# Three edits to the order of work around the routing stage of an attention and mixture-of-experts kernel: running sums one unit of projections sooner, one unit more behind the fifth group of one-hot rows, last keys' activations one product later

## The chip, the cores and the metric

The kernel runs on one core of one Trainium2 chip. The metric is the device time of one execution in microseconds (us). The core has five engines that run their own instruction streams in order and wait for each other by semaphores: PE (TensorE, the matrix products; its weight loads are shown as PEld), DVE (VectorE), ACT (ScalarE), POOL (GpSimd) and SP (SyncE, which only issues DMAs here). ACT and POOL issue DMAs too.

## The reference, cut to what matters

The input x has 2 x 2048 tokens of 512 channels. It is normalised, xn = layernorm(x); the attention layer normalises xn once more with gamma and beta.

```python
# attention, on xn, causal, one head of width 512
x_norm = (xn - mu) / sqrt(var + EPS) * gamma + beta
q, k, v = x_norm @ Wq, x_norm @ Wk, x_norm @ Wv
s = softmax(mask(q @ k.T / sqrt(512))) @ v @ o_proj + xn
# mixture of 8 experts on xn, the best 2 of each token
scores = xn @ gate_w.T + gate_b + bias
top_scores, top_idx = top_k(scores, 2)
comb = sum(one_hot(top_idx, 8) * softmax(top_scores))
h = silu(einsum('td,ehd->teh', xn, w1) + b1)
y = einsum('teh,edh->ted', h, w2) + b2
out = x + s * silu(einsum('ted,te->td', y, comb))
```

## The kernel before, in words

**Stages.** The tokens are cut into 32 tiles of 128, and the tiles into 8 blocks of 512 tokens (`NB` = 8). The first stage, to about 256 us, normalises each block, turns it so that the channels lie on the partitions (`zT`), applies gamma and beta (`kT`, the keys), and multiplies it by two folded weights: `wqk` (query times key weights) and `wvo` (value times output weights). The results go to DRAM. In the same stage the scores of the experts are made, and near its end the routing: each token's two experts, its place in the list of its expert, and the inverse list `toki`, which says which token lies in which slot. From about 256 to 570 us the experts run over the slots, whose rows POOL gathers by `toki`. The rest is attention and the output.

**Products.** The projections of blocks 0 to 6 use seven products of half size in place of eight. `items` lists (block, weight) pairs, 14 of them, and `chain_of_products` gives the order (i, k) of the products: the seven k of neighbouring items are interleaved, so that a bank's copies lie behind another product. `one_product(i, k)` issues four matmuls of 128 x 256 in float32 into one of four PSUM banks (`bank_a` to `bank_d`, line 465) and then ACT's copies:

- k = 1 writes bank_a. k = 2 adds to bank_a, which is copied out (line 491).
- k = 5 writes bank_d, which ACT copies to a tile `p5` (line 488, `FIFTH`).
- k = 6 adds to bank_b, and ACT copies bank_b to bank_c (line 494).
- k = 3 adds to bank_b, which is copied out (line 478), and bank_b is loaded with the next item's bank_a (line 499). k = 7 and k = 4 add to bank_c (lines 478 and 508).

The outputs of k = 3 and k = 7 still lack the fifth product. DVE adds it (line 330), an instruction that `deferred` holds back until two more products have been issued (`add_due`).

**Units.** The generator `pieces` yields after one or two products, four units for seven products; the units of block 7 are whole products instead, four matmuls of 128 x 512 (lines 381 and 386). There are 64 units. Whatever is put in between is placed by counting units: `next(projected)` issues one more. The instructions stand in the program in just this order (`manual_schedule`), so an engine meets its work in the order in which the Python code issued it.

**Keys.** `keys(b)` turns a block with DVE copies (line 307), and puts the four activations `scaled` (ACT, line 312), one for each quarter of the channels, into `pending`, with the number of the product from which they may be issued. After each product `scale_next` issues one that is due. The last of the four also issues the DMA that stores the keys to `kt_d`, on ACT's queue.

**Routing.** `route()` is a generator. It starts when 41 of the 64 units are out, and each `yield n` lets n more units be issued before it goes on. First come constants (POOL, lines 531 to 556) and the choice of the two experts (DVE, lines 566 to 595), which ends with the matrix `chosen`. Then two small matmuls, `cum` and `tot_p` (lines 599 and 601), give running sums over the tokens of a tile and sums of each tile, and about 30 DVE instructions (lines 603 to 673) make from them the slot of each choice. Then the inverse list: for each of the two choices (k = 0, 1) and each of four groups of eight tiles (t0 = 0, 8, 16, 24), DVE builds one-hot rows `at`, `mine` and `which` (lines 706 to 717), and `invert()` issues eight bf16 matmuls on PE that add the group into `inv_p` (line 684). The fifth group is k = 1, t0 = 0. The tiles `at` and `which` lie in the pool `hot` with two buffers, so the third group after a given one can be built only when PE has used the given one. After the last group `inv_p` is turned into `toki` (line 731), and POOL gathers the first slots (line 883).

```python
groups.append((at, which, k, t0))
if k == 0 or t0 + GROUP < NT:
    yield 1
invert()
```

The lines of `route` up to its end consume 4 + 5 + 4 + 3 + 1 = 17 units; the rest of the 64 are issued with the first steps of the experts.

Of the kernel before, what the change touches and what calls it, by code (L numbers as in the profile page):

```python
# [26 lines left out]
def gated_attention_moe(  # L27
# [35 lines left out]
    NB = NT // BT  # L63
# [231 lines left out]
    def keys(b):  # L295
        zs = zs_of.pop(b)
        zT = ztp.tile([P, ND, TB], F32, name=f"zT_{b}", tag="zT")
        kT = kp.tile([P, ND, TB], F32, name=f"kT_{b}", tag="kT")
        if b < BY_TE:
            for c in range(ND):  # L300
                pt = ps_t.tile([P, TB], F32, name=f"pz_{b}_{c}", tag="pt")
                for t in range(BT):
                    nc.tensor.transpose(pt[:, ts(t, P)], zs[t][:, ts(c, P)], ident)
                nc.scalar.copy(zT[:, c, :], pt)
        else:
            for t in range(BT):
                nc.vector.tensor_copy(
                    zT[:, :, ts(t, P)].bitcast(U16).rearrange("p c (t h) -> p c t h", h=2),
                    zuts.pop((b, t)).rearrange("p (h c) t -> p c t h", h=2),
                )  # L310
        def scaled(c):
            nc.scalar.activation(
                kT[:, c, :], zT[:, c, :], AF.Identity,
                scale=gam[:, c : c + 1], bias=bet[:, c : c + 1],
            )
            if c == ND - 1:
                nc.scalar.dma_start(out=kt_d[b], in_=kT)

        wait = made[0] + (3 if b in (1, NB - 1) else 6)
        pending.extend((wait, scaled, c, b) for c in range(ND))  # L320
        if b < BY_TE:
            scale_all()
        kts[b], zts[b] = kT, zT

    made, pending, deferred = [0], [], []
# [11 lines left out]
    def scale_all():  # L337
        while pending:
            _, f, c, _ = pending.pop(0)
            f(c)  # L340
# [179 lines left out]
    def route():  # L520

        with ExitStack() as rt:
# [46 lines left out]
            def over_e(dst, src, op):  # L569
                nc.vector.tensor_reduce(dst, src.rearrange("p e t -> p t e"), AX.X, op)  # L570
# [23 lines left out]
            chosen = rp.tile(G, BF16, name="chosen")  # L594
            nc.vector.tensor_tensor(chosen, oh1, oh2, ALU.add)
            flat = chosen.rearrange("p e t -> p (e t)")
            yield 4
            cum = ps_r.tile([P, E * NT], F32, name="cum")
            nc.tensor.matmul(cum, lhsT=tri, rhs=flat, start=True, stop=True)
            tot_p = ps_r.tile([P, E * NT], F32, name="tot_p")  # L600
# [80 lines left out]
            def invert():  # L681
                at, which, k, t0 = groups.pop()
                for i in range(GROUP):
                    nc.tensor.matmul(
                        inv_p, lhsT=at[:, i, :], rhs=which[:, i, :, :],
                        start=(k == 0 and t0 + i == 0), stop=(k == 1 and t0 + i == NT - 1),
                    )

            for k, oh in enumerate((oh1, oh2)):
                nc.vector.tensor_tensor(oh, oh, excl, ALU.mult)  # L690
                pos = rp.tile([P, NT], F32, name=f"pos{k}")
                over_e(pos, oh, ALU.add)
                nc.vector.tensor_copy(posi[k], pos)
                parts_i = rp.tile([P, 2, NT], I32, name=f"parts_i{k}")
                nc.vector.tensor_scalar(
                    parts_i[:, 0, :], posi[k], 7, None, ALU.arith_shift_right
                )
                nc.vector.tensor_scalar(parts_i[:, 1, :], posi[k], P - 1, None, ALU.bitwise_and)
                part = rp.tile([P, 2, NT], BF16, name=f"part{k}")
                nc.vector.tensor_copy(part, parts_i)  # L700
                for t0 in range(0, NT, GROUP):
                    def along(v, n):
                        return v[:, t0 : t0 + GROUP].unsqueeze(2).to_broadcast([P, GROUP, n])

                    at = hot.tile([P, GROUP, P], BF16, name=f"at_{k}_{t0}", tag="at")
                    nc.vector.tensor_tensor(  # L706
                        at, lane.unsqueeze(1).to_broadcast([P, GROUP, P]),
                        along(part[:, 1, :], P), ALU.is_equal,
                    )
                    mine = hot.tile([P, GROUP, NSP], BF16, name=f"mine_{k}_{t0}", tag="mine")  # L710
                    nc.vector.tensor_tensor(
                        mine, slot_b.unsqueeze(1).to_broadcast([P, GROUP, NSP]),
                        along(part[:, 0, :], NSP), ALU.is_equal,
                    )
                    which = hot.tile([P, GROUP, 2, NSP], BF16, name=f"which_{k}_{t0}", tag="which")
                    for i in range(2):
                        nc.vector.tensor_tensor(
                            which[:, :, i, :], mine, along(tok[i], NSP), ALU.mult
                        )
                    groups.append((at, which, k, t0))  # L720
                    if k == 0 or t0 + GROUP < NT:
                        yield 1
                    invert()
            yield 1
            inv = rp.tile([P, 2, NSP], F32, name="inv")
# [62 lines left out]
    for b in range(1, NB):  # L788
        at = begin[b]
        put(at, keys, b)  # L790
        put(at + 3, both, b)
        put(at + (4 if b == NB - 1 else 7), keep_scores, b)
        if b > 1:

            before = begin[b - 1] if b > 2 else 0
            put(max(before - 1, 0), norm_stats, b)
            put(before + 1, norm_roots, b)
            put(before + 1, norm_rows, b)
            if b + 2 < NB:

                put(before + 4, load, b + 2)
# [17 lines left out]
    norm(0)  # L819
    fold(wqk, parts[0], parts[1], 1.0 / math.sqrt(KEY))  # L820
    keys(0)
    key_sums(0)
    weight_sums(wqk, "q")
# [68 lines left out]
    for n in route():  # L892
        for _ in range(n):
            next(projected)
            done += 1
            for f, args in between.pop(done, []):
                f(*args)
            sum_keys(done)
            if done >= W2_FROM:
                load_w2(w2_left.pop(0))  # L900
# [430 lines left out]
    for i in range(NS):  # L1331
# [21 lines left out]
        for _ in range(3):  # L1353
            if i >= paired.stop and early:
                f, b, c = early.pop(0)
# [303 lines left out]
    for s in range(NT + OUT + 2):  # L1659
# [15 lines left out]
        for k in range(NT):  # L1675
            if k not in AHEAD:
                wait = 4 - k % 2 if k // 2 in FAST else 3
# [162 lines left out]
```

## Time and profile before

| | |
|---|---|
| three runs | 1026.64, 1028.63, 1025.37 us; median 1026.64 |
| the profiled execution | 1028.63 us, of which the span from first to last instruction is 1026.9 |
| mean granted PE clock | 0.998 of full speed |
| busy PE, DVE, POOL, ACT | 1015.6, 713.9, 479.9, 408.9 us |
| moved by DMA | 209.42 MB, 204 GB/s on average |

The busy time is a share of the span. A busy PE alone says nothing of the stage; the waits of PE, the chain of waits that ended last, and the windows of PE's clock say where it stood still or ran slowly. Times inside the program are in us from the start of the span.

### The profile page before, as it was taken

The numbers are of one execution on the slowest core, as the hardware profiler recorded it, in microseconds if no ns is written. First come the engines' busy times: TensorE is split into PE (matmuls) and PEld (weight loads), VectorE is DVE, ScalarE is ACT, GpSimd is POOL, SyncE is SP. The second block draws the span as 40 slices with busy tenths as digits, with TensorE's granted clock in tenths as the row PEclk, the third lists the DMA queues.
The fourth block names the chain that finished last, engine by engine and source line by source line (L and its number), as shares of the span: only waits on it lengthen the run. The fifth ranks groups of instructions, "written<-read, shape, count | busy, mean of one in ns | idle before, by whom it ended". The sixth has DMA issues, their size and how long they took to land.

```text
span 1026.9 us, 13492 instructions
## 1 busy us (share of the span) xinstructions
PE 1015.6 (99%) x3956; PEld 666.4 (65%) x3956; DVE 713.9 (70%) x1395; ACT 408.9 (40%) x817; POOL 479.9 (47%) x479
## 2 busy tenths in 40 slices
PE   9999999989999999999999999999999999999998
PEld 5688887864577667766754347687675544447577
DVE  5777746795887777677734559787577556888667
ACT  3344444322444444354445322122335553542341
POOL 3364564003744444444431237254556776754272
PEclk9999999999999999999999999999999999999999
DMA  8698995988899999999999567454768769653371
GB/s 297 204 260 287 294 276 239 343 276 184 189 231 219 203 215 223 189 228 216 221 200 237 158 208 168 110 123 136 201 174 238 230 189 251 186 136 116 97 162 42
DMA packets 299367, 209.42 MB, mean 204 GB/s; under 512 B 234392, under 2 KB 247448, under 8 KB 298272
## 3 DMA queue, kind: packets, MB, share of 16 engines
q1 hardware_dynamic: 283840, 156.09, 61.4%
q0 software_dynamic: 10560, 35.17, 13.1%
q10 hardware_dynamic: 4896, 17.30, 4.5%
q8 instruction: 34, 0.56, 0.2%
q14 instruction: 37, 0.30, 0.1%
HBM read 92.89 MB, written 60.03 MB: 149 GB/s over the span
## 4 chain that ended last, share of the span: by engine, by line
PE 90%; DVE 3%; issue 3%; SPq 1%; DMA 1%; POOL 1%; ACT 0%; ACTq 0%; POOLq 0%; DVEq 0%
PE py L1107 15%; PE ps L1219 13%; PE p L1482 12%; PE p L1050 10%; PE p L1271 8%; PE po L1434 6%; PE bank_a L465 4%; PE bank_b L465 4%; PE bank_c L465 4%; PE p L1434 3%; PE bank_d L465 2%; PE ph L998 2%; DMA y_d<-y 1%; PE bank_a L219 1%; DVE at L706 1%
## 5 line engine op out<-in xcount | busy, mean ns | idle before, releaser
L1107 PE MATMUL py<-arena,ht 128*128 (+3 forms) x408 | 182.3, 593 | 0.0
L1219 PE MATMUL ps<-k,q 128*128 128x512 f32 (+3 forms) x416 | 143.0, 495 | 0.0
L1394 POOL COPY pu<-pT 128x1024 uint16<-128x1024 uint16 (+2 forms) x74 | 82.4, 1147 | 118.3 <-ACT pT L1384 58.6
L1078 POOL COPY hu<-h 128x704 uint16<-128x704 uint16 x68 | 63.0, 946 | 155.9 <-issue 121.6
L1107 PEld LDWEIGHTS py<-arena,ht 128*128 128x128 f32 (+3 forms) x408 | 73.3, 183 | 82.2 <-issue 77.2
L1219 PEld LDWEIGHTS ps<-k,q 128*128 128x128 f32 x416 | 74.6, 190 | 66.8 <-issue 57.4
L883 POOL DMA_INDIRECT xs<-zu_d,toki x68 | 79.5, 1169 | 72.7 <-DVE toki L731 57.8
L1093 ACT ACTIVATE ht<-ht,b1sel 128x128 f32<-128x128 f32 (+3 forms) x228 | 71.1, 378 | 99.0 <-DVE ht L1087 99.0
L1057 DVE TENSOR_TENSOR h<-p,h 128x176 f32<-128x176 f32 x182 | 55.5, 337 | 53.8 <-PE p L1050 50.0
L1577 POOL DMA_INDIRECT yg<-y_d,posi x64 | 67.7, 1059 | 36.6 <-DVE yg L1588 21.1
L1434 PE MATMUL po<-v,pT 128*128 128x512 f32 x152 | 67.8, 592 | 0.0
L280 POOL COPY zu<-z 128x1024 uint16<-128x1024 uint16 x32 | 38.0, 1187 | 60.8 <-DVE z L265 60.8
L1384 ACT ACTIVATE pT<-pT,nm 128x1024 f32<-128x1024 f32 x14 | 16.1, 1148 | 110.2 <-DVE nm L1307 71.2
L1416 DVE COPY pT<-puT 128x1024 uint16<-128x1024 uint16 (+2 forms) x74 | 53.3, 749 | 7.6 <-DMA puT<-pu 7.5
L1115 ACT COPY y<-py 128x512 f32<-128x512 f32 x55 | 32.1, 584 | 59.7 <-PE py L1107 44.2
L1384 ACT ACTIVATE pT<-ps,nm 128x512 f32<-128x512 f32 (+3 forms) x52 | 30.0, 581 | 61.3 <-DVE nm L1307 37.6
L958 DVE COPY xT<-xhT 128x1024 uint16<-128x1024 uint16 x68 | 47.0, 713 | 6.2 <-DMA xhT<-xs 5.7
L1277 DVE TENSOR_TENSOR pT<-p,pT 128x512 f32<-128x512 f32 x49 | 32.8, 686 | 26.0 <-PE p L1271 22.3
L1434 PEld LDWEIGHTS po<-v,pT 128*128 128x128 f32 x152 | 28.6, 190 | 31.9 <-issue 30.1
L1606 POOL TENSOR_TENSOR o<-o,yg 128x512 f32<-128x512 f32 x30 | 41.4, 1381 | 14.3 <-DVE o L1598 14.2
L1087 DVE COPY ht<-huT 128x768 uint16<-128x768 uint16 x68 | 39.4, 579 | 12.5 <-DMA huT<-hu 12.2
L1598 DVE SCALAR_TENSOR_TENSOR o<-xo,xscale,o 128x512 f32<-128x512 f32 x30 | 27.3, 918 | 28.7 <-ACT o L1595 28.7
(323 smaller groups left out, 2159.3 us busy)
## 6 DMA issues: line engine op xcount, KB each, us to landing
y_d<-y SPq DMA_DIRECT2D x68, 256.0 KB
zu_d<-zu SPq DMA_DIRECT2D x32, 264.0 KB
kt_d<-kT ACTq DMA_DIRECT2D x8, 1024.0 KB
k<-kt_d SPq DMA_DIRECT2D x32, 256.0 KB
q<-qt_d SPq DMA_DIRECT2D x32, 256.0 KB
v<-v_d SPq DMA_DIRECT2D x32, 256.0 KB
xo<-in_x_dram SPq DMA_DIRECT2D x32, 256.0 KB
x<-in_x_dram SPq DMA_DIRECT2D x30, 256.0 KB
```

What stands on the lines that cost most here:

```text
L465: nc.tensor.matmul(ps[:, r, :], lhsT=lhs[:, c, ts(r, P)], rhs=rhs[:, c, :], start=(start and r + c == 0), stop=(c == 1), skip_group_check= ...
L883: nc.gpsimd.indirect_dma_start(out=xs, out_offset=None, in_=zu_d, in_offset=bass.IndirectOffsetOnAxis(ap=toki[:, order[i] : order[i] + 1], ...
L1050: nc.tensor.matmul(ps, lhsT=x[:, c], rhs=y(c).rearrange("p o h -> p (o h)"), start=(c == 0), stop=(c == ND // 2 - 1),)
L1078: nc.gpsimd.tensor_copy(hu[:, :, :H], h.bitcast(U16).rearrange("p (d h) -> p h d", h=2))
L1093: nc.scalar.activation(ht[:hn, c, at], ht[:hn, c, at], AF.Silu, bias=b1sel[:hn, c, j : j + 1])
L1107: nc.tensor.matmul(py[at, :], lhsT=ht[:k, c, at], rhs=rhs[n], start=(c == 0), stop=(c == NH - 1),)
L1219: nc.tensor.matmul(ps[:, :w], lhsT=aqs[seq[s] // 2][:, c, ts(t % 2, P)], rhs=aks[first + j][:, c, :w], start=(c == 0), stop=(c == ND - 1),)
L1271: nc.tensor.matmul(ps, lhsT=x[:, c], rhs=y[:, c], start=(c == 0), stop=(c == ND // 2 - 1))
L1394: nc.gpsimd.tensor_copy(pu[:, : 2 * w].rearrange("p (h d) -> p h d", h=2), turned[s][:, k : k + w].bitcast(U16).rearrange("p (d h) -> p h ...
L1434: nc.tensor.matmul(dst, lhsT=turned[s][:, ts(k, P)], rhs=avs[first + k // BT][:, k % BT, cols], start=(start and k == k0), stop=(k == k1 - 1),
L1482: nc.tensor.matmul(dst, lhsT=a[:, k], rhs=v(k), start=(k == 0), stop=(stop and k == n - 1))
L1577: nc.gpsimd.indirect_dma_start(out=y, out_offset=None, in_=y_d, in_offset=bass.IndirectOffsetOnAxis(ap=posi[k][:, n : n + 1], axis=0),)
```

## The change

The change moves work and adds or removes none. It has three places.

```diff
@@ keys(b)
-        wait = made[0] + (3 if b in (1, NB - 1) else 6)
+        wait = made[0] + {1: 3, NB - 1: 4}.get(b, 6)
@@ route(), behind `chosen`
-            yield 4
+            yield 3
             cum = ps_r.tile([P, E * NT], F32, name="cum")
@@ route(), the groups of one-hot rows
                     if k == 0 or t0 + GROUP < NT:
-                        yield 1
+                        yield 2 if k + t0 == 1 else 1
                     invert()
```

The first lets the activations of the last block's keys be issued from the fourth product after `keys(7)` on, where it was the third. The second lets three units be issued between `chosen` and the two small matmuls of the running sums, where it was four. So everything behind them in `route` stands one unit sooner, until the third place: after the rows of the fifth group (k + t0 is 1 only for k = 1, t0 = 0) two units are issued before its matmuls, where it was one. Groups five to eight stand where they stood, and the units consumed by `route` are 3 + 5 + 4 + 4 + 1 = 17 as before.

In the instructions as built, the streams of POOL and SP are in the same order. On PE, `cum` and `tot_p` stand ahead of two products that they stood behind, groups one to four stand one unit sooner, and two products on bank_b, k = 6 and k = 3 of the last item, follow each other with no group in between. On DVE the two adds of p_10 (line 330) come behind the running sums in place of ahead of them, and the two of p_12 behind the rows of the fourth group in place of ahead of them. On ACT the copy of line 494 comes ahead of the first activation of block 7's keys, and the fourth of them, with its DMA, behind the copies of lines 355 and 478.

## The prediction

> **What bounds the kernel now.** I read, in this order, the busy shares and the chain of waits of the page, then the waits of PE alone between 140 and 275 us, then the timeline there. The first two say that PE is the bound over the whole span:
>
> ```profile
> PE 1015.6 (99%) x3956; PEld 666.4 (65%) x3956; DVE 713.9 (70%) x1395; ACT 408.9 (40%) x817; POOL 479.9 (47%) x479
> ...
> PE 90%; DVE 3%; issue 3%; SPq 1%; DMA 1%; POOL 1%; ACT 0%; ACTq 0%; POOLq 0%; DVEq 0%
> ```
>
> So an edit counts only if it changes a time in which PE stands still, or PE's clock. The waits of PE in the stage of the change (us in all, times, longest):
>
> ```profile
> PE inv_p L684 <- DVE which L717: 2.2, 1, 2.2
> PE bank_b L465 <- ACT bank_c L494: 1.4, 2, 1.2
> PE bank_c L465 <- ACT so L478: 0.3, 1, 0.3
> ```
>
> The long one of the second kind, in the timeline (start, length, engine, then idle time before it and who ended it):
>
> ```profile
> 163.71 0.81 ACT L312 ACTIVATE kT<-zT,bet,gam 128x512 f32<-128x512 f32 x1 [3.11 <-DVE zT L307]
> ...
> 164.43 0.57 ACT L494 COPY bank_c<-bank_b 128x512 f32<-128x512 f32 x1
> ...
> 165.06 1.99 PE L465 MATMUL bank_b<-arena,kT 128*128 128x256 f32 x8 [1.19 <-ACT bank_c L494]
> ```
>
> ACT stands 3.11 us before a key activation that needs zT from DVE, and the copy that PE needs stands behind it. The other wait, in the chain and in PE's clock (PEclk, third column from the right):
>
> ```profile
> 228.00 1.37 DVE which L717 x2
> 229.37 0.04 issue
> 229.41 0.63 PE inv_p L684 x8
> 230.05 5.18 PE bank_c L381 x8
> 235.23 3.43 PE bank_d L381 x8
> ```
>
> ```profile
> 230.00:231.00 1.00, 1.00 (x4) 0.36 (x4) 0.85 (x4) 0.00 (x0) 0.00 (x0) 0.81 1.02 410
> 231.00:232.00 1.00, 1.00 (x3) 0.48 (x2) 0.96 (x2) 0.00 (x0) 0.83 (x1) 0.50 0.56 213
> ...
> 233.00:234.00 1.00, 1.00 (x2) 0.34 (x2) 0.97 (x2) 0.00 (x0) 1.00 (x1) 0.50 0.64 148
> 234.00:235.00 1.00, 1.00 (x3) 0.38 (x2) 0.93 (x3) 0.00 (x0) 0.69 (x2) 0.98 0.66 177
> ```
>
> DVE builds one-hot rows without a pause up to 229.36 (26.5 us busy of the 28 from 198 to 226), PE waits 2.16 us for the eighth group, and then runs at half clock: the first unit takes 5.18 where the next takes 3.43, so 1.75 us more. From 255.7 to 556 PE then never waits, so what is won before 255.7 is kept.
>
> **What the Trainium skill says.** "TensorE: Matmul & The Clock Gate", Part 1 (the HAM clock gate), says that the array falls to half clock after an idle window of about 3.4 us, counted in windows that run free of the kernel. The trace agrees on the half (0.50) and about on its length, but a gap of 2.16 us was enough here, while the gap of 1.36 us at 163.7 left the clock at 1.00. The same page's "Architectural detail" calls ACT and DVE strict FIFO; the ACT lines above agree.
>
> **The change, part by part.** All times are on the clock of the profiled execution. Durations are its own; I lay them in the order in which the changed program stands on each engine.
>
> *Key activations one product later.* In ACT's order the copy L494 now comes ahead of all four activations of b = 7. Its source is ready near 161.7 (PE left it at 161.54), so it ends near 162.3, before PE wants it at 161.97 + 1.73 = 163.70. The wait 163.70 to 165.06 goes: 1.36, and with it the slower start of the next product (1.92 to the next start instead of 1.73, 0.19): **1.55 us** sooner for PE. What is late next: the fourth activation and its DMA kt_d on ACT's queue come behind the copy of bank_c, ending near 169.7 instead of 169.0. The units of b = 7 read it from 223 on, so they do not feel it; POOL's constants (L531, 170.81 now) reuse its space, so they start near 169.8, 1.0 sooner and not 1.55. DVE's choice of experts hangs on them: `chosen` ends at 181.24 - 1.0 = 180.2.
>
> *Running sums one unit sooner.* cum and tot_p (0.11 us each) move ahead of two products (2 x 1.73 = 3.45). Now they start at 186.07, 4.8 us after `chosen`; then at 186.07 - 3.45 - 1.55 = 181.1, still 0.9 after `chosen`, so PE gets no new wait. DVE's running sums (186.49 to 195.69, 9.2 us) end near 190.7, 5.0 sooner. But their successors are then late: the two adds of the fifth product (L330 on so_10, 1.3 us, moved behind the sums), and the two of p_11, of which the second needs ACT's copy of bank_c, 195.13 + 0.59 = 195.72 now, 194.15 then. L690 follows 0.6 later: near 194.75 instead of 196.81. So DVE gains **2.1**, not 5.0. The moved adds feed a store that waits for both at 194.08 now; they are done at 192.0, so ACT's queue is not held.
>
> *Groups 1 to 4 one unit sooner on PE.* Group 1 comes to 205.29 - 3.45 - 1.55 = 200.3, its rows end at 201.91 - 2.1 = 199.8: no wait. Groups 2, 3, 4 come to 204.2, 206.5, 210.4; their rows are ready at 203.0, 206.2 and 209.4 (the adds of p_12, 1.2 us, move behind group 4). `hot` has two buffers, so DVE's third group waits for group 1 on PE: 0.89 us at 205.96 now, nothing then (group 1 is through at 201.0, DVE comes at 203.0). DVE gains **0.9** more, 3.0 in all. Both new margins of 0.3 to 0.5 us bound the error: at worst 0.5 is lost, at best nothing.
>
> *One unit more behind the fifth group.* With no group between the last two products on bank_b, PE sees the whole copy chain between them: 0.2 + 0.57 + 0.06 = 0.84 us idle, where a group of 0.47 stood in part of it. Queued behind: everything on PE, and so group 5, which comes near 218.7 (its rows are ready at 215.7). DVE's seventh group needs group 5 through, 218.7 + 0.47 + 0.2 = 219.4, and arrives at 222.35 - 3.0 = 219.35. No row of before shows this wait; I take **0.1** lost, between 0 and 0.6 (PE's starts there are good to some half us). The end of the rows is then 229.36 - 2.9 = 226.4; PE comes to the eighth group near 225.9, so it still waits, some 0.6 us, and the group starts **2.95 us** sooner, near 226.45.
>
> *Clock.* A gap of 0.6 us, and 0.84 at 214.8, are both below the 1.36 that left the clock alone: the 1.75 us of half clock go. Sum on the profiled execution: 2.95 + 1.75 = **4.7 us**.
>
> *Behind it.* The order on SP and POOL is the same, with the same DMAs. toki comes 2.95 sooner, PE's first expert product 4.7 sooner (251.0). xT for it is ready at 244.47 + 0.76 now, so 8 us of slack remain after losing 1.75. The DMA-laden stage from 516 to 570, where PE waits 1.4 us, is paced by PE's own progress: zero, with 1 us either way.
>
> **Time.** The profiled execution took 1028.63, of which 1026.9 is span: 1028.63 - 4.7 = 1023.9. It is the slowest of three runs; the others, 1026.64 and 1025.37, are lower by about what the half clock costs or more. If they lack it (an estimate, since their clock is not shown), the median gains 2.95: 1023.7. Over such runs, one in three with the half clock, the gain is 2.95 + 0.6 = 3.5 us off a mean of 1026.88, 1023.3. I take **1023.5**.
>
> **Rivals.** Measurements of this kernel can tell about 0.3%, 3.1 us, from no change; 1023.56 is that edge below, 1029.7 above.
> - *Forecast* (0.66): as worked out, 1022.0 to 1025.3. The edge lies inside it, just above the point: 0.44 below, 0.22 above.
> - *The gap closes wholly* (0.14): rows reach PE in time for group 8, or stalls of 516 to 570 shrink by 1 us. 0.6 to 1.6 us more: 1022.4. For it speaks that two 0.3 margins are only estimates; against it, DVE has no idle time left to lose between L690 and the last row.
> - *The gain is eaten* (0.08): PE's lateness at group 5 passes to DVE, and the gap stays above the level that halves the clock. Only the first 1.55 or so is left: 1025.1.
> - *Slower* (0.12): the clock halves at the new 0.84 us wait before the second product on bank_b at 214.8, because the small bf16 groups and transposes near it count little. 1.75 us lost there go through group 5 to DVE's seventh group and so to group 8, and its gap halves the clock a second time: 1026.64 - 2.95 + 3.5 = 1027.2. Each further half-clock window adds 1.75, since a late PE makes the next gap; two more give 1030.7. It decides from some 1 us of idle time in one window; against it stands the 1.36 us without effect.
> - That the moves do not happen is excluded: the instructions as built stand in the order used above.
>
> **How the numbers follow.** Faster by over 0.3%: 0.44 + 0.14 = 0.58. Slower by over 0.3%: 0.07, the part of the last rival with more than two such windows. Within: 0.22 + 0.08 + 0.05 = 0.35. Range: 1020.8 to 1027.2, which takes the closed gap with the spread of the runs (1.6 below) at one end and the slower rival's first value at the other.
>
> **What would show it.** In the profile after: no PE wait on bank_c near 165; `tot` near 181.5; L690 near 194.8; no idle time before the third `at`; an idle PE of some 0.8 before a bank_b product near 215; the eighth group near 226.5 after a gap under 1 us; PEclk 1.00 through 235 and seven units of 3.43; the first expert product near 251. I am wrong if the clock halves, if DVE waits over 0.6 for group 5, or if the 4.7 us are no longer there at 516 or at 570.

## The result, and the profile after

The changed kernel took 1022.8 us (median of 7 runs, 1021.88 to 1025.76) against 1028.1 us of the kernel before beside it (7 runs, 1025.37 to 1030.15). The ratio is 0.996, with a 95% interval of 0.9942 to 0.9979: faster by 0.4%. In a later set of runs it took 1022.29 (7 runs) against 1026.91 (46 runs), ratio 0.9946 [0.9926, 0.9967]. The ratio is not the quotient of the two medians, which is 0.9948 and 0.9955. The profiled execution took 1024.79 us, of which 1023.1 is span, where that of before took 1028.63 and 1026.9.

PE is still busy for 99% of the span, by the page of the changed kernel (busy shares; chain of waits by engine):

```profile
PE 1013.5 (99%) x3956; PEld 666.2 (65%) x3956; DVE 712.2 (70%) x1395; ACT 408.9 (40%) x817; POOL 482.1 (47%) x479
...
PE 89%; DMA 4%; issue 3%; DVE 2%; POOL 1%; ACT 1%; SPq 1%; POOLq 0%; DVEq 0%; ACTq 0%
```

The busy time of PE fell by only 2.1 us, and that is the half clock (1.7) and little else: the rest of the gain was idle time, which this row does not show. The waits of PE between 140 and 275 us do (us in all, times, longest), in the changed kernel:

```profile
PE bank_b L465 <- ACT bank_c L494: 0.7, 1, 0.7
PE inv_p L684 <- DVE which L717: 0.4, 1, 0.4
PE bank_c L465 <- ACT so L478: 0.3, 1, 0.3
```

The wait for `which` shrank from 2.2 to 0.4. The wait for the copy L494 is halved: of the two of before, that near 165 is gone, and the short one near 216 has grown from 0.24 to 0.71, since the group that stood ahead of it has left (timeline of before, then of the changed kernel):

```profile
216.38 1.99 PE L465 MATMUL bank_b<-arena,kT 128*128 128x256 f32 x8 [0.24 <-ACT bank_c L494]
```

```profile
214.92 1.99 PE L465 MATMUL bank_b<-arena,kT 128*128 128x256 f32 x8 [0.71 <-ACT bank_c L494]
```

The timeline around 163 shows how the first went (start, length, engine; in brackets idle time before):

```profile
161.56 0.57 ACT L494 COPY bank_c<-bank_b 128x512 f32<-128x512 f32 x1 [1.20 <-PE bank_b L465]
...
161.74 1.89 PE L465 MATMUL bank_a<-kT,wqk 128*128 128x256 f32 x8
...
163.47 1.89 PE L465 MATMUL bank_b<-arena,kT 128*128 128x256 f32 x8
163.47 1.52 ACT L312 ACTIVATE kT<-zT,bet,gam 128x512 f32<-128x512 f32 x2 [1.34 <-DVE zT L307]
```

The copy now runs ahead of the key activation, ACT's wait for zT comes behind it, and the second product on bank_b starts with no idle time in front. The chain of waits of the changed kernel, with the longer wait near 215 and the eighth group:

```profile
214.30 0.58 ACT bank_c L494
214.88 0.04 issue
214.92 1.99 PE bank_b L465 x8
...
226.23 0.63 PE inv_p L684 x8
226.86 3.49 PE bank_c L381 x8
230.34 3.43 PE bank_d L381 x8
```

The eighth group starts at 226.23 in place of 229.41, and the unit behind it takes 3.49 in place of 5.18. The windows say why (last three columns: PE's clock, DMA share, GB/s):

```profile
228.00:230.00 2.00, 2.00 (x6) 0.95 (x5) 1.93 (x3) 0.00 (x0) 1.70 (x2) 1.00 1.02 401
230.00:232.00 2.00, 2.00 (x6) 0.86 (x5) 1.90 (x4) 1.23 (x2) 1.70 (x2) 1.00 0.63 164
```

The clock is 1.00 right behind the group, where the kernel before had a stretch at 0.50. In this trace, as in the forecast, the change is one wait removed, one wait shortened, one short wait lengthened, and one unit at full clock.

### The profile page after: what moved, and what is told of

Same layout as the page of the kernel before. It is cut to its first block, busy times and chain, and to the rows that moved or that the text cites. A ratio compares the mean times of both kernels' runs of the same rounds, so it can differ in the third digit from the quotient of the medians.

```text
span 1023.1 us, 13492 instructions
## 1 busy us (share of the span) xinstructions
PE 1013.5 (99%) x3956; PEld 666.2 (65%) x3956; DVE 712.2 (70%) x1395; ACT 408.9 (40%) x817; POOL 482.1 (47%) x479
## 4 chain that ended last, share of the span: by engine, by line
PE 89%; DMA 4%; issue 3%; DVE 2%; POOL 1%; ACT 1%; SPq 1%; POOLq 0%; DVEq 0%; ACTq 0%
PE py L1107 15%; PE ps L1219 12%; PE p L1482 12%; PE p L1050 10%; PE p L1271 8%; PE po L1434 6%; PE bank_a L465 5%; PE bank_b L465 5%; PE bank_c L465 5%; PE p L1434 3%; PE bank_d L465 2%; PE ph L998 2%; DMA y_d<-y 1%; DMA raw<-in_qkv_t_dram 1%; PE pg L347 1%
```

## The experiments

**How they are read.** The device times of one kernel spread over some 4 us and more, so I read each step in the trace first. Below is the start of the same ACT instruction against its start in the trace of the kernel before. What was already there at 47 us is taken off, because executions begin their first products up to 1.6 us apart (0.23 us sooner in the changed kernel's trace, 1.41 later in that of `e2_sums`). Negative is sooner. At 205 us the rows with the second edit are 0.52 later than without it, since PE has by then done one group of about 0.5 us more.

| kernel | 193 us | 205 us | 235 us | 323 us | 671 us |
|---|---|---|---|---|---|
| changed | -1.75 | -1.22 | -4.65 | -4.72 | -4.25 |
| changed, again | -1.75 | -1.22 | -4.65 | -3.52 | -5.79 |
| `e1_keys` | -1.75 | -1.74 | -3.44 | -1.56 | -3.83 |
| `e2_sums` | 0.00 | +0.52 | -2.91 | -1.76 | -4.03 |
| `e3_unit_at_end` | -1.74 | -1.22 | -2.05 | -2.12 | -0.36 |
| `e4_fill16` | -0.01 | -0.01 | -1.70 | +1.05 | -1.22 |
| `e5_fill6` | 0.00 | 0.00 | -1.70 | -1.77 | -4.04 |
| `e6_last_add` | -1.75 | -1.22 | -5.24 | -4.80 | -7.01 |
| `e7_long_gap` | -0.02 | -0.02 | +2.51 | +2.45 | +1.26 |
| `e8_adds_11` | -1.74 | -1.22 | -4.64 | -4.71 | -6.98 |

Up to 235 us the rows repeat to 0.02 where the programs agree. The last two columns don't; more on that below. Note that the trace of before has the half clock, so a row with full clock gains 1.70 at 235 for that alone.

### The first edit alone

```diff
-        wait = made[0] + (3 if b in (1, NB - 1) else 6)
+        wait = made[0] + {1: 3, NB - 1: 4}.get(b, 6)
```

> The first edit alone: key activations of block 7 one product later, sums and groups as before. My theory: the wait of PE near 165 (1.36 us, with the slower start 1.55) goes. DVE gains as much, not only PE, since the sums start 1.55 sooner (`chosen` has 4.8 us to spare), ACT's copy of bank_c that holds L690 comes 1.55 sooner, and so does group 1 that holds the third `at`. So PE and DVE reach the eighth group 1.55 sooner alike: the gap there stays near 2.2 us, the unit behind it stays at half clock (5.2 us), and the first expert product starts 1.55 sooner: about 1.5 us off the median. Rival A (the clock carries the whole gain): nothing at the end, the 1.55 turns into a longer gap of 3.7 us because DVE does not follow. Rival B: with the wait near 165 gone the clock at 230 stays full too, and the whole 4.7 us comes from this edit.

Measured: 1025.12 us (22 runs) against 1026.8 (59 runs), ratio 0.9977 [0.9963, 0.999]. The gap is as long as before, but what follows is not slow (waits, then timeline, of `e1_keys`):

```profile
PE inv_p L684 <- DVE which L717: 2.2, 1, 2.2
```

```profile
228.55 0.63 PE L684 MATMUL inv_p<-which,at 128*128 128x136 bf16 x8 [2.16 <-DVE which L717]
229.02 3.65 PE L381 MATMUL bank_c<-kT,wqk 128*128 128x512 f32 x8
```

The wait near 165 is worth 1.75 us, and DVE follows in full, so rival A falls. But the same gap of 2.16 us, to the hundredth, left the clock at 1.00 here (one of the windows of `e1_keys`), which my theory had excluded:

```profile
230.00:232.00 2.00, 2.00 (x6) 0.89 (x5) 1.93 (x4) 0.00 (x0) 1.44 (x1) 1.00 0.35 133
```

Rival B falls as well: the mean clock of 10 of the 22 runs is 0.998, of the other 12 it is 1.000. One unit at half clock takes about that off the mean (half of 3.4 us in 1027 is 0.0017). So the half clock is a draw, and this trace drew the other side. Most runs have no trace, so from here on a mean clock of 0.998 or less stands for the half clock; it marks it, and does not show where it fell.

### The second and third edit alone

```diff
-            yield 4
+            yield 3
...
-                        yield 1
+                        yield 2 if k + t0 == 1 else 1
```

> The second and third edit without the first: sums one unit sooner, one unit more behind the fifth group, key activations as before. My theory: the wait near 165 (1.36 us) is back. The sums start at 186.07 - 3.45 = 182.6, but L690 waits for ACT's copy of bank_c near 195.7, so DVE gains 0.5 there and 0.9 at the third `at`: 1.4 us. PE comes to the eighth group after a gap of about 0.6 us in place of 2.2, the clock stays at 1.00, the unit behind it takes 3.43 in place of 5.18. First expert product 1.4 + 1.75 = 3.15 us sooner than in the kernel before, about 3 us off the median; with the first edit alone this adds up to the whole change. Rival A: the two parts need each other, without the first edit the gap stays near 2 us and the clock halves: 0 to 1.4 us off. Rival B: these two edits carry all of it, 4.7 us, and the first edit nothing.

Measured: 1024.98 us (14 runs), ratio 0.9989 [0.997, 1.0008], so alone not distinct from the kernel before by the ratio; the median is 1.8 us lower, where about 3 were expected. The timeline of `e2_sums`:

```profile
229.61 0.63 PE L684 MATMUL inv_p<-which,at 128*128 128x136 bf16 x8 [0.43 <-DVE which L717]
230.08 3.65 PE L381 MATMUL bank_c<-kT,wqk 128*128 128x512 f32 x8
```

The gap is 0.43, and the clock full: 2.91 sooner at 235 (3.15 expected), of which 1.70 is the clock and 1.2 is the shorter gap less the longer wait near 215. Without the clock the two halves add up in the trace: 1.75 (first edit) and 1.2 make 2.95, and the changed kernel has 4.65 - 1.70 = 2.95. Neither needs the other.

### The spare unit behind the last group

```diff
-                        yield 2 if k + t0 == 1 else 1
+                        yield 1
                     invert()
-            yield 1
+            yield 2
```

> The first and second edit, but the spare unit stands behind the last group in place of behind the fifth: all eight groups one unit sooner on PE. My theory: the third edit is what turns DVE's gain into time. DVE builds the last rows at about the same time as in the changed kernel (near 226.1), PE comes to groups 5 to 8 up to 3.4 us sooner and only waits: 4 to 4.5 us of waits for `which` in the stage in place of 0.4, the largest over 1 us. The eighth group starts near 226.1, one unit more is behind it, so the first expert product comes 3.3 us later than in the changed kernel, and 5.0 later if the gap halves the clock: 0 to 1.6 us off the median of the kernel before. Rival: groups that come sooner set DVE free sooner (`hot` has two buffers), and the rows end well ahead of 226; then this kernel is as fast as the changed one or faster, 1022 to 1023.

Measured: 1028.71 us (14 runs), ratio 1.0012 [0.9991, 1.0034]: the gain is gone. The median lies 1.9 us above the kernel before, where 0 to 1.6 below it was expected; its trace also lost 1.8 us more than that of before between 323 and 671 us. The waits of PE in `e3_unit_at_end`:

```profile
PE inv_p L684 <- DVE which L717: 3.8, 2, 2.8
```

PE comes sooner and waits 3.8 us for DVE's rows in place of 0.4. In this trace the clock stayed full after 2.8 us of idle time, but 8 of the 14 runs have a mean clock of 0.998 or less. The rival falls, though not wholly: the eighth group does start 0.8 us sooner than in the changed kernel (225.77 less 0.14 is 225.63, against 226.23 and 0.23), and 0.6 of that is DVE's last add, which in this trace stands behind the rows. But one unit more of 3.4 us stands behind the group. The third edit does not help DVE; it puts a unit of PE's work where PE would otherwise wait.

### The gap filled with other matmuls

```diff
                     if k == 0 or t0 + GROUP < NT:
                         yield 1
+                    else:
+                        for _ in range(16):
+                            nc.tensor.matmul(cum, lhsT=tri, rhs=flat, start=True, stop=True)
                     invert()
```

> The kernel before with 16 repeats of the small matmul `cum` (0.11 us each, 1.76 us in all, same values into the same place) ahead of the eighth group's matmuls, in PE's gap of 2.16 us there. No wait is taken away and no work moved. My theory (the half clock costs 1.75 us by itself): PE is busy in the gap, the clock stays at 1.00 at 230 to 235, the unit behind the group takes 3.43 in place of 5.18, and the first expert product starts 1.75 us sooner at the same start of the eighth group (229.4): about 1.5 us off the median. Rival A: the clock falls anyway (small bf16 matmuls count little, or it isn't the gap): no change, or up to 0.1 slower. Rival B: the half clock is there only in some runs: a gain of 0.5 to 1 us in the median, and no half clock in this profile or in that of the kernel before beside it.

Measured: 1026.19 us (22 runs) against 1026.8, ratio 0.9999 [0.9981, 1.0017]. The timeline of `e4_fill16`:

```profile
227.64 1.91 PE L725 MATMUL cum<-chosen,tri 128*128 128x256 bf16 x16
229.97 0.63 PE L684 MATMUL inv_p<-which,at 128*128 128x136 bf16 x8 [0.42 <-DVE which L717]
230.44 3.65 PE L381 MATMUL bank_c<-kT,wqk 128*128 128x512 f32 x8
```

The group starts when it started (229.97 less the 0.56 of this run's start is 229.41), and the unit behind it is 1.70 sooner through: the half clock costs 1.70 of its own. That the filling keeps the clock this one trace can't show, since `e1_keys` had the full clock with the gap open. The counts do: 2 of 22 runs have a mean clock of 0.998 or less, against 24 of 59 without the filling. In the median it is worth 0.6 us, as rival B had it and not the 1.5 of my theory; the interval can't tell that from nothing, and 1.70 in 4 of 10 runs would be 0.7. With 6 repeats in place of 16:

> The kernel before with 6 small repeats of `cum` in the gap at the eighth group (some 0.7 us), where the earlier run had 16: the idle time left is some 1.5 us in place of 2.16 or 0.42, the start of the group the same. My theory: whether PE's clock halves behind a gap is a draw whose odds rise with the idle time. A run with one halved unit has a mean clock of 0.998 or less: 24 of 59 runs of the kernel before and 10 of 22 with the first edit alone (gap 2.16 in both), 2 of 22 with 16 repeats (gap 0.42). With 1.5 us I expect the halved clock in 5 to 30 in 100 runs and a median within 0.7 us of the one with 16 repeats. Rival (a threshold of idle time somewhere under 2.16 decides it): none at all, or as often as at 2.16. Second rival (the small matmuls don't count, the clock is an accident): 4 in 10.

Measured: 1026.76 us (20 runs) against 1026.91 (46 runs), ratio 0.9996 [0.9983, 1.0008]. The timeline of `e5_fill6`:

```profile
229.95 0.63 PE L684 MATMUL inv_p<-which,at 128*128 128x136 bf16 x8 [1.50 <-DVE which L717]
```

At 1.5 us of idle time 1 run of 20 has the lower mean clock, and that one took 1032.81 us, so something else may have lowered it. On the same chip 22 of 46 runs of the kernel before have it, so the second rival falls and the odds rise between 1.5 and 2.2 us; whether they are small or nothing at 1.5 these runs can't tell.

### A long gap

```diff
-                    if k == 0 or t0 + GROUP < NT:
+                    if k == 0 or t0 + 2 * GROUP < NT:
                         yield 1
                     invert()
-            yield 1
+            yield 2
```

> The kernel before with the unit that stands ahead of the seventh group's matmuls moved behind the eighth: PE comes to the seventh group 3.4 us sooner and waits for DVE there and at the eighth, some 5.6 us idle in all, cut only by eight small matmuls (0.6 us). The rows and `toki` come when they came. My theory: after such idle time the clock halves in nearly all runs (mean clock 0.998 or less in 8 of 10 or more), and the first expert product starts 3.4 us later than in a run of the kernel before with full clock behind the gap, plus 1.75 or more for the half clock: median 3 to 6 us above the kernel before. Rival (the clock is an accident that doesn't depend on the gap): the half clock in 4 of 10 runs as before, median 3.4 us above. Second rival (units are paid back, since xT for the first products is late anyway): less than 2 us above.

Measured: 1030.43 us (20 runs) against 1026.91, ratio 1.0033 [1.002, 1.0045]. All 20 runs have a mean clock of 0.998 or less; the 3.5 us in the median fit the first rival (3.4) as well, so it is this count that speaks against it. The timeline and one of the windows of `e7_long_gap`:

```profile
226.13 0.63 PE L684 MATMUL inv_p<-which,at 128*128 128x136 bf16 x8 [2.36 <-DVE which L717]
229.29 1.07 PE L684 MATMUL inv_p<-which,at 128*128 128x136 bf16 x8 [2.53 <-DVE which L717]
230.16 4.64 PE L381 MATMUL bank_b<-kT,wqk 128*128 128x512 f32 x8
```

```profile
230.00:232.00 2.00, 2.00 (x7) 0.97 (x5) 1.50 (x5) 0.00 (x0) 0.52 (x1) 0.50 0.00 0
```

The two gaps are 4.9 us, not 5.6, because DVE's add on p_13 went behind the rows with the unit. By the mean clock the half clock comes every time, and in the trace it begins ahead of the eighth group's matmuls already (1.07 in place of 0.63). That the draw depends on the idle time is shown by the counts: 1 of 20 at 1.5, 46 of 105 (kernel before, both chips) and 10 of 22 (`e1_keys`) at 2.16, 20 of 20 here.

### DVE's last add behind the last rows

```diff
         while units:
-            add_due(0)
+            add_due(0 if len(units) < 8 else 9)
             unit(*units.pop(0))
-            while unstored:
+            while unstored and not deferred:
```

> The changed kernel, and DVE's last fifth-product add (L330 on p_13, 0.6 us, at 222.33) behind the rows of the eighth group in place of ahead of them; its store on ACT's queue one unit later. My theory: after the change the eighth group still waits 0.43 us for DVE's chain, of which this add is the last piece that need not be there. The rows end 0.6 sooner, PE finds them ready, the wait for `which` at 226.2 is gone, the first expert product starts 0.4 us sooner than in the changed kernel; the median moves by less than can be measured, 1022.0 to 1023. Rival: DVE's chain is held by something else at this place (group 5 through the two buffers of `hot`), and the rows end where they did: the wait of 0.43 stays.

Measured: 1022.04 us (8 runs) against 1026.91, ratio 0.9949 [0.993, 0.9969]; the changed kernel beside it 1022.29. The timeline of `e6_last_add`:

```profile
225.71 1.11 PE L684 MATMUL inv_p<-which,at 128*128 128x136 bf16 x16
...
251.17 9.11 PE L998 MATMUL ph<-w,xT 128*128 x30 [0.27 <-POOL keep L1326]
```

Groups seven and eight now follow each other without a gap, so the wait of 0.43 was DVE's chain, as said, and the 235 us column has 5.24. But PE then stands a moment before its first expert product, by the trace for a mask that POOL makes, and that product starts only 0.2 us sooner than in the changed kernel, where 0.4 was expected (251.17 less 0.32 and 0.23 of different starts is 250.62, against 250.78). Of the kernels with several runs it has the lowest median, but it is not distinct from the changed one.

### The adds of p_11 later

```diff
-            deferred.append((made[0], nc
+            deferred.append((made[0] + (3 if i == 11 else 0), nc
```

> The changed kernel with the two adds of p_11 (L330) due five products after their bank and not two, so that they stand on DVE behind the rows of groups 1 and 2 and no longer between the running sums and L690. In the changed kernel DVE waits 0.58 and 1.03 us there for ACT's copies of the two banks. My theory: these waits are why DVE gained 2.4 us at L690 and not the 5.4 us by which the sums start sooner. Without them L690 starts near 191.4 in place of 194.37 (counted from the start of the same stage), 3.0 sooner: 1.6 of waits and 1.3 of adds that come later. But it brings nothing at the end, since DVE's seventh group must find the fifth used by PE (`hot` has two buffers): DVE's waits before `at` for PE grow from 0.16 to about 1.6 us in all, the eighth group waits 0.4 us as before and starts near 226.2. Rival: with the waits gone DVE's whole chain moves up 1.6 us, the eighth group's wait is gone, and the first expert product comes 0.4 us sooner than in the changed kernel.

One execution: 1021.82 us. The waits of DVE between 178 and 230 us, in the changed kernel and then in `e8_adds_11`:

```profile
DVE arena L330 <- ACT arena L478: 1.6, 2, 1.0
...
DVE at L706 <- PE inv_p L684: 0.2, 1, 0.2
```

```profile
DVE at L706 <- PE inv_p L684: 1.4, 2, 0.9
...
DVE so L330 <- ACT so L478: 0.4, 1, 0.4
```

The wait for ACT's copies is exchanged for waits for PE's groups. L690 starts at 191.77, or 191.39 on the clock of the changed kernel's trace (this run's start is 0.38 later), 3.0 sooner as expected, and the eighth group at 226.24 on that clock, where it was. The rival falls: behind L690 it is the two buffers of `hot` that bound DVE.

## Why the prediction was right, and where it was not

The forecast was faster, 1023.5 within 1020.8 to 1027.2; measured was 1022.8. Most of the steps hold to a few tenths (trace times of the changed kernel, whose start is 0.23 sooner than that of before):

- *Key activations*: 1.55 expected, 1.75 measured, in the changed kernel as in the first edit alone.
- *Running sums*: `tot` near 181.5 expected, at 181.06; L690 near 194.75, at 194.37. DVE's gain of 2.1 there is 2.44 - 0.23 = 2.2. That ACT's copies of the banks set this and not the sums is what `e8_adds_11` shows.
- *Third `at`*: no wait, as expected. *Bank_b near 215*: 0.84 expected, 0.71 measured, 0.53 of it lost to PE. *Seventh group's wait for group 5*: 0.1 expected, 0.16 measured.
- *Eighth group*: 2.95 sooner expected, 3.18 - 0.23 = 2.95 measured, after a gap of 0.43 for 0.6.
- *Sum at the first expert product*: 4.7 expected; 4.88 - 0.23 = 4.65 measured.

Of the rivals, the closed gap comes nearest in time (1022.4 expected) but not in mechanism: the gap did not close, and `e6_last_add` shows that closing it brings next to nothing. The slower one fell: with its wait of 0.71 the changed kernel shows no half clock near 215, nor does any of the other four traces with this wait (one of the windows of the changed kernel):

```profile
216.00:220.00 4.00, 3.74 (x24) 3.11 (x23) 3.81 (x6) 1.17 (x2) 0.00 (x0) 1.00 0.92 329
```

The range held, but two steps failed.

*The clock.* The prediction reasoned that a gap of 2.16 us halves the clock and one under 1.36 does not. (Of the gap near 163.7 only 1.19 us are idle time by the line that it shows; 1.36 is how much later the next product starts.) Yet its sum supposed that two of three runs with the same gap lacked the half clock, and put the share at one in three, from three times; that this came near the truth is luck. It is a draw: 46 of 105 runs of the kernel before have a mean clock of 0.998 or less, and the trace of `e1_keys` has the same gap at full clock. "TensorE: Matmul & The Clock Gate" of the Trainium skill, Part 1, says that the clock is set by windows of about 3.4 us that run free of the program. That fits: where a window begins differs from run to run, and the gap counts only by what of it falls into one window. An estimate from that page's 3.4 and the counts here: if a window must be idle for T, a gap of 2.16 does it in a share of (3.4 + 2.16 - 2T) / 3.4 of runs; 46 of 105 gives T of about 2.0 us. Then 1.5 us should never do it (measured 1 of 20), and 2.8 us in about 0.6 of runs (`e3_unit_at_end`, 8 of 14). This reading fits the counts but is not shown by itself: no run shows the windows. For the sum it means that 2.95 us are there in each run and 1.70 in 0.44 of them, 3.7 on average, where the prediction had 3.5. (In the device times the 46 runs of the kernel before with the lower mean clock are slower than the other 59 by 0.8 us in the median and 1.1 in the mean, less than 1.70; the draws below blur this.)

*What lies behind 255 us.* The prediction took it that what is won before 255.7 us is kept. The stage from 516 to 570 us was priced at zero, with 1 us either way, since PE's own progress was thought to pace it. Between 323 and 671 us the kernel before lost, in its trace, 2.27 us that seven of the ten traces in the table did not lose (their last two columns differ by 2.2 to 2.3); the changed kernel lost 2.7 in its first trace and none in its second. The stage from 255 to 323 us does the same: `e4_fill16` gave back 2.75 us there, the first trace of the changed kernel nothing. Both places are waits for what is made from the gathered rows (`xT`, `ht`, `h`), and they come or stay away without regard to the edit, as the two traces of the same changed kernel show. A third wait, for DVE's `pT` near 823 us, cost 0.65 and 0.87 us in these two traces and nothing in the other nine; two traces can't tell whether that is chance. Of the signs of being wrong, the third therefore came in part: of the 4.7 us, 4.7 were there at 510 us and 4.25 at 583 in the first trace, 3.5 and 5.8 in the second. The gain of 4.65 us at 235 is blurred by draws of 1 to 4 us, and the 3.8 us between the two profiled spans is not a better measure of the change than the 4.65.

What stays open: the medians differ by 5.3 and by 4.6 us, and 3.7 are accounted for. The intervals of the ratio, 2.2 to 6.0 us and 3.4 to 7.6, both hold 3.7. For the later set of runs I had expected a ratio near 0.9965, and had named 0.9954 or less as the sign that the whole 4.7 us come in each run; it was 0.9946, so this expectation was missed. The counts speak against that reading, since 59 of 105 runs of the kernel before show no half clock that could go. Among the runs with a mean clock above 0.998 alone the medians are lower than the kernel before by 1.7 us (`e1_keys`), 1.8 (`e2_sums`) and 3.7 (changed kernel, 7 runs against 24), where the traces without the clock give 1.75, 1.2 and 2.95. The rest may be those later draws, or the changed kernel may meet them less often; with 14 runs of it this isn't settled. The two halves of the change measured 1.7 and 1.8 us in their medians, 3.5 together, which speaks for chance.

## What to carry to other kernels

Where one engine is busy all the time, look for the engine that feeds it at the end of the stage, and follow a gain through each engine's queue: sums that started five microseconds sooner were worth two, because an add behind them waited for another engine's copy, and with that wait gone two buffers held the engine instead. Leave a unit of independent work of the bound engine for the place where it would wait; without that, work that comes sooner only waits longer. And judge a change of a few tenths of a per cent by the starts of the same instructions in two traces, counting by many runs what in them is a draw.

## What had not been expected of the hardware

- The same idle gap of PE (2.16 us) halved its clock for about 3.4 us in the trace of before and left it alone in that of `e1_keys`; by the mean clock it did so in 46 of 105 runs of the kernel before. At 1.5 us it was 1 of 20, at 2.36 and 2.53 us close together 20 of 20. One such stretch cost 1.70 us.
- Small bf16 matmuls of 0.11 us, 16 of them in the gap, were enough to keep the clock in most runs: 2 of 22 have a mean clock of 0.998 or less in place of 24 of 59.
- Executions start their first products up to 1.6 us apart, two of the changed kernel 1.26 (from 23 to 150 us the kernels here agree but for that), so that a raw span mixes this with what an edit did.
